# Squared key norms from the diagonal of k kᵀ on VectorE instead of TensorE transposes and ScalarE squares

## The chip, the cores and the metric

The kernel runs on one core of one Trainium2 chip. A core has five engines that work side by side and wait for one another through semaphores: TensorE (PE in the profile; its weight loads are PEld), VectorE (DVE), ScalarE (ACT), GpSimd (POOL) and SyncE (SP, which here issues DMAs). The metric is device time in microseconds (us), lower is better. TensorE writes its products to PSUM, eight banks of 512 fp32 values per partition; VectorE and ScalarE read them from there.

## The reference

The reference is one transformer block over 8 sequences of 256 tokens and 256 channels, all in fp32: a layer norm with a scale and shift from a conditioning vector, a gated delta-rule attention with 16 key heads and 32 value heads of width 128, then a second layer norm and a feed-forward part that keeps two of every four hidden values. Cut to what matters here:

```
qkv = x @ W_qkv.T ; z = x @ W_z.T ; beta = sigmoid(x @ W_b.T) ; decay = exp(-softplus(..) * exp(A_log))
q, k, v = causal convolution of qkv over 4 tokens, per channel
q, k = q / |q|, k / |k|                       # per token and key head
S = S * decay + k (beta * (v - k S))          # per token, two value heads to a key head
out = q S ; out = rmsnorm(out) * norm_w * silu(z) ; y = out @ W_out.T
```

The norm |k| that is to be computed is one number per token and key head: the root of the sum of 128 squares.

## The kernel before

The scan over tokens is done in chunks of 128 tokens. For each key head, two sequences and two chunks (so four 128x128 blocks), the kernel builds a triangular matrix from k kᵀ, the decays and beta / |k|², inverts it, and gets the outputs by matmuls. The heads go in groups of four, and the sequences in pairs: 4 pairs x 4 groups = 16 groups, 64 key heads in all.

The names that matter:

- `stage_a` (L479) makes one key head: `projected` (L429) multiplies the weights with the tokens into the PSUM tile `ps_k`; `convolved` (L417) makes `k_t` of it, one ScalarE and three VectorE instructions. `k_t` has channels on partitions and tokens along the free axis, so a sum over channels is a sum over partitions.
- `norms2` (L441) gives the squared norms. It transposes the four blocks on TensorE into a bank (`ps_n2k`), so that tokens are on partitions, and squares each on ScalarE with an accumulated sum (`junk`, L451). It serves the queries too (`n2q`).
- From the squared norms `n2` come a clamp (L500), a reciprocal (L505), `bk` = beta / |k|² (L507), and on GpSimd `diag` (L516), which puts `bk` on the diagonals of eight blocks, and `nk`, the norm (L523).
- Then k kᵀ, the tile `ps_kk` (L534), a scan over `dbc` (the decays, loaded by DMA) and `diag` into `e` (L553), and the product `a_t` = k kᵀ times `e` (L565). Four DMAs write the diagonal blocks of `a_t` to `scr` in DRAM (L574).
- `stage_b` (L582) loads the blocks of a whole group back (`blk`), and solves 32x32 blocks in 30 steps on VectorE (L599, L605). `levels` (L669) joins them to whole inverses on TensorE (`ps_w`, `ps_t`, `ps_w2`, `ps_t2`), `attend` (L759) computes the outputs, `prepare` (L614) queries, values and gates, `shares` (L894) the output projection, `feed_forward` (L160) the last part (`ps_ff`, `ps_out`).

The parts are Python generators. Each `yield` hands over to the next, and `along` (L1084) advances the next group's `stage_a` and `stage_b` while the present group attends. That gives a first order. From it a scheduler makes the final order on each engine when the program is built: earlier text has precedence, and an instruction that is not ready in its model lets later ones pass. So an edit in one place can shift the order elsewhere. [...]

PSUM is split in three pools: `ps_in` with three banks (`ps_k`, `ps_qv`, `ps_z`, `ps_y`, and the transposes of `norms2`), `ps_inv` with two (`ps_kk`, the four tiles of `levels`, `ps_ff`, `ps_out`), `ps_mix` with three for `attend`. A tile holds its bank from its first write until its last reader is done. `diag` has one buffer (pool `single`).

In the first group (`first`) nothing runs beside `stage_a`; there `e` is made in another way (L536 to L551).

## Time and profile before

| | |
|---|---|
| median of 3 runs | 2170.34 us (2168.94 to 2173.52) |
| profiled execution | 2170.51 us, span of the instructions 2168.7 us |
| mean granted TensorE clock | 0.991 of full speed |
| TensorE busy | 2068.7 us, 95% of the span |
| VectorE busy | 1669.4 us, 77% |
| ScalarE busy | 1379.5 us, 64% |
| GpSimd busy | 370.3 us, 17% |

The page lists busy time by engine, the chain of work that ended last, and groups of instructions by line, with the shape, the count, the busy time in us, the mean duration of one in ns, and the idle time of the engine just before them with what ended it. The durations of matmuls overlap, since they are pipelined. An ordinary fp32 matmul of this kernel stands in the trace as two records and a transpose as one: the 256 products of k kᵀ are 512 records, the 256 transposes of keys 256. The line numbers in the profile before are those of the code above.

### The profile page before, as it was taken

What the parts mean: (1) busy time and instruction counts of PE and PEld (TensorE: products, weight loads), DVE (VectorE), ACT (ScalarE), POOL (GpSimd) and SP (SyncE); (2) the same over time, 40 slices, a digit from 0 to 9 for tenths busy, and PEclk for the clock granted to TensorE, in tenths of its full rate; (3) what the DMA queues carried; (4) which work ended last, traced back from release to release, by engine and by line L of the source; (5) the groups of instructions that cost most, each with busy time, mean ns of one, the idle gap of its engine ahead of it and who ended that gap; (6) DMA issues with size and microseconds to landing.
All of it is one profiled execution on the core that took longest, in us unless ns stands there. A gap on an engine that the chain in (4) does not pass through costs nothing.

```text
span 2168.7 us, 46393 instructions
## 1 busy us (share of the span) xinstructions
PE 2068.7 (95%) x16684; PEld 1633.8 (75%) x16684; DVE 1669.4 (77%) x4039; ACT 1379.5 (64%) x4552; POOL 370.3 (17%) x375
## 2 busy tenths in 40 slices
PE   8889999899999999999999999999999999999998
PEld 5567777777777787777777787777778777777887
DVE  6678786787869587797877868787887868878457
ACT  3577677766656566665666656667666666666652
POOL 3120212112120211212121121211212021120010
PEclk9999999999999999999999999999999999999999
DMA  4242424223242443434334343433434244343226
GB/s 142 86 112 64 106 70 111 76 82 111 80 113 71 114 129 91 130 92 105 119 87 112 106 124 97 118 113 89 125 92 116 83 119 128 94 112 91 72 90 212
DMA packets 324517, 226.85 MB, mean 105 GB/s; under 512 B 254520, under 2 KB 266168, under 8 KB 324288
## 3 DMA queue, kind: packets, MB, share of 16 engines
q1 hardware_dynamic: 304416, 163.34, 28.0%
q10 hardware_dynamic: 19872, 60.54, 8.7%
q8 instruction: 133, 2.18, 0.4%
q14 instruction: 96, 0.79, 0.1%
HBM read 186.28 MB, written 29.12 MB: 99 GB/s over the span
## 4 chain that ended last, share of the span: by engine, by line
PE 50%; DVE 12%; DMA 7%; ACT 7%; issue 3%; POOL 1%; SPq 1%; DVEq 0%; ACTq 0%; POOLq 0%
PE ps_z L641 7%; PE ps_y L902 7%; PE ps_qv L432 6%; PE ps_ks L813 4%; PE ps_ff L190 3%; DVE cv L420 3%; DMA blk<-scr 2%; PE ps_o L832 2%; PE ps_out L244 2%; PE ps_k L432 2%; PE ps_u L848 2%; DMA scr<-a_t 2%; PE ps_u L805 1%; PE ps_o L854 1%; PE ps_gt L888 1%
## 5 line engine op out<-in xcount | busy, mean ns | idle before, releaser
L420 DVE SCALAR_TENSOR_TENSOR cv<-ps_qv,conv_sb,cv 128x510 f32<-128x510 f32 (+2 forms) x564 | 408.2, 735 | 29.8 <-ACT cv L418 28.2
L432 PE MATMUL ps_qv<-h_bp,wh 128*128 128x512 f32 x768 | 369.0, 605 | 20.5 <-DVE cv L420 8.0
L105 POOL TENSOR_TENSOR rs<-ss,minus_halves 128x4 f32<-128x4 f32 x128 | 134.3, 1055 | 1104.2 <-DVE ss L859 1096.9
L641 PE MATMUL ps_z<-wh,h_bp 128*128 128x256 f32 x1024 | 247.4, 386 | 10.6 <-ACT junk L451 7.4
L902 PE MATMUL ps_y<-wo,og_p 128*128 128x256 f32 x1024 | 236.1, 380 | 0.0
L432 PEld LDWEIGHTS ps_qv<-h_bp,wh 128*128 128x128 f32 x768 | 132.9, 191 | 125.3 <-issue 97.0
L641 PEld LDWEIGHTS ps_z<-wh,h_bp 128*128 128x128 f32 x1024 | 187.9, 192 | 38.5 <-ACT junk L451 9.6
L902 PEld LDWEIGHTS ps_y<-wo,og_p 128*128 128x128 f32 x1024 | 187.9, 190 | 22.3
L599 DVE TENSOR_TENSOR tmp<-blk,xb 128x30 f32<-128x30 f32 (+14 forms) x480 | 157.3, 328 | 51.2 <-ACT xb L593 41.7
L839 ACT ACTIVATE junk<-o 128x128 f32<-128x128 f32 x512 | 154.2, 306 | 54.8 <-DVE o L855 44.3
L516 POOL TENSOR_TENSOR diag<-consts,bk 128x1032 f32<-128x1032 f32 x64 | 122.8, 1918 | 364.1 <-DVE bk L507 364.1
L418 ACT ACTIVATE cv<-ps_qv,conv_sb 128x512 f32<-128x512 f32 x188 | 129.7, 690 | 82.8 <-PE ps_qv L432 81.4
L553 DVE TENSOR_TENSOR_SCAN e<-dbc,diag 128x1032 f32<-128x1032 f32 x60 | 138.0, 2300 | 37.1 <-POOL diag L516 35.5
L605 DVE TENSOR_TENSOR xb<-xb,tmp 128x30 f32<-128x30 f32 (+14 forms) x480 | 157.6, 328 | 9.5
L872 DVE SCALAR_TENSOR_TENSOR og<-o,rs,gz 128x128 f32<-128x128 f32 x512 | 146.2, 349 | 14.5 <-POOL rs L105 13.9
L420 DVE SCALAR_TENSOR_TENSOR k_t<-ps_k,conv_sb,k_t 128x510 f32<-128x510 f32 (+1 forms) x189 | 139.4, 739 | 20.6 <-ACT k_t L418 18.8
L813 PE MATMUL ps_ks<-u,cross 128*128 128x128 f32 x1024 | 141.3, 282 | 0.9 <-ACT u L807 0.9
L813 PEld LDWEIGHTS ps_ks<-u,cross 128*128 128x128 f32 x1024 | 132.1, 196 | 11.1 <-issue 4.8
L190 PE MATMUL ps_ff<-h,w_ff 128*128 128x128 f32 x1024 | 131.9, 278 | 3.3 <-ACT h L149 2.4
L779 ACT ACTIVATE vn<-ps_v,nk 128x256 f32<-128x256 f32 x256 | 104.0, 483 | 44.6 <-PE ps_v L774 44.1
L190 PEld LDWEIGHTS ps_ff<-h,w_ff 128*128 128x128 f32 x1024 | 123.1, 192 | 7.6 <-ACT h L149 3.3
L432 PE MATMUL ps_k<-h_bp,wk 128*128 128x512 f32 x256 | 122.3, 602 | 1.2 <-ACT junk L451 1.2
(177 smaller groups left out, 4280.1 us busy)
## 6 DMA issues: line engine op xcount, KB each, us to landing
wh<-in_w_heads ACTq DMA_DIRECT2D x64, 640.0 KB, 4.0
w_ff<-in_w_ff SPq DMA_DIRECT2D x128, 256.0 KB, 3.1
dbc<-d_dram SPq DMA_DIRECT2D x60, 516.0 KB, 4.6
wo<-in_w_heads ACTq DMA_DIRECT2D x32, 512.0 KB, 3.7
w_dn<-in_w_down SPq DMA_DIRECT2D x64, 256.0 KB, 3.3
wk<-in_w_keys SPq DMA_DIRECT2D x16, 512.0 KB, 4.9
scr<-a_t SPq DMA_DIRECT2D x256, 32.0 KB, 2.5
blk<-scr SPq DMA_DIRECT2D x16, 512.0 KB, 3.6
```

The source lines that it names most:

```text
L105: nc.gpsimd.tensor_tensor(out=out, in0=in_, in1=minus_halves[:, :n], op=ALU.pow)
L190: nc.tensor.matmul(ps[:, a, l, :], lhsT=w[:, k, l, :], rhs=h2[:, k, :], start=(k == 0), stop=(k == CC - 1),)
L420: nc.vector.scalar_tensor_tensor(out=dst[:, :, d:], in0=ps[:, :, : T - d], scalar=taps[:, KC - 1 - d : KC - d], in1=dst[:, :, d:], op0=ALU ...
L432: nc.tensor.matmul(ps.rearrange("p b t -> p (b t)"), lhsT=w[k], rhs=h_bp[:, k, :], start=(k == 0), stop=(k == CC - 1),)
L553: nc.vector.tensor_tensor_scan(e.rearrange("p i s t -> p (i s t)"), dbc.rearrange("p i f -> p (i f)"), diag.rearrange("p s t -> p (s t)"), ...
L599: nc.vector.tensor_tensor(out=tmp, in0=blk[:, j, j + 1 :, None].to_broadcast([P, m, j]), in1=xb[:, j, None, 0:j].to_broadcast([P, m, j]), ...
L605: solved = nc.vector.tensor_tensor(out=xb[:, j + 1 :, 0:j], in0=xb[:, j + 1 :, 0:j], in1=tmp, op=ALU.subtract)
L641: nc.tensor.matmul(ps[:, n, :], lhsT=h_bp[:, k, i * T + n * P : i * T + (n + 1) * P], rhs=wh[:, k * 640 + 384 : (k + 1) * 640], start=(k = ...
L813: nc.tensor.matmul(ps_ks[:, ct, h, :], lhsT=cross[:, h, ct, :], rhs=u0[:, h, :], start=True, stop=True)
L839: nc.scalar.activation(junk, o[:, n, h, :], AF.Square, accum_out=ss[:, n, h : h + 1])
L872: nc.vector.scalar_tensor_tensor(out=og[:, n, h, :], in0=o[:, n, h, :], scalar=rs[:, 2 * n + h : 2 * n + h + 1], in1=gz[:, i, n, h, :], op ...
L902: nc.tensor.matmul(ps_y[:, n, :], lhsT=og_p[:, j // 2, i, n, j % 2, :], rhs=wo[:, j // 2, j % 2, :], start=(j == 0), stop=(j == 3),)
```

## The change

k kᵀ of a head is computed ahead of its norm, for all heads. For the heads after the first group (60 of 64) the squared norms are read from its diagonal: VectorE multiplies the four blocks with the identity into the first part of `diag`'s buffer (`own`), and sums each row. The clamp, the reciprocal and all that follows are as they were, and GpSimd then overwrites the same buffer with the `diag` proper. The four heads of the first group keep `norms2`, and so do the queries. The tile `diag` is asked for earlier; its size and its one buffer are the same. `a_t` reads the same PSUM tile as before (`kk` is `ps_kk`).

```diff
             yield rec
-            n2 = norms2(k_t, "n2k")
+            ps_kk = bank(ps_inv, [P, 2 * NCH, P], "ps_kk")
+            for i in range(2):
+                for n in range(NCH):
+                    kc = k_t[:, i, n * P : (n + 1) * P]
+                    nc.tensor.matmul(ps_kk[:, i * NCH + n, :], lhsT=kc, rhs=kc, start=True, stop=True)
+            kk = ps_kk
+            diag = single.tile(
+                [P, 2 * NS, PE1], F32, tag="dbc" if first and kh % 2 else "diag", name="diag"
+            )
+            if first:
+                n2 = norms2(k_t, "n2k")
+            else:
+
+                n2 = small.tile([P, 2, NCH], F32, tag="n2k", name="n2k")
+                own = diag[:, : 2 * NCH, :P]
+                nc.vector.tensor_tensor(
+                    out=own, in0=kk, in1=ident[:, None, :].to_broadcast([P, 2 * NCH, P]), op=ALU.mult
+                )
+                nc.vector.tensor_reduce(
+                    out=n2.rearrange("p i n -> p (i n)"), in_=own, axis=AX.X, op=ALU.add
+                )
             nc.vector.tensor_scalar_max(n2, n2, L2_EPS2)
...
-            diag = single.tile(
-                [P, 2 * NS, PE1], F32, tag="dbc" if first and kh % 2 else "diag", name="diag"
-            )
             done = nc.gpsimd.tensor_tensor(
...
             rec["e"] = e
-            ps_kk = bank(ps_inv, [P, 2 * NCH, P], "ps_kk")
-            for i in range(2):
-                for n in range(NCH):
-                    kc = k_t[:, i, n * P : (n + 1) * P]
-                    nc.tensor.matmul(ps_kk[:, i * NCH + n, :], lhsT=kc, rhs=kc, start=True, stop=True)
...
-                    in0=ps_kk[:, i * NCH : (i + 1) * NCH, None, :].to_broadcast([P, NCH, 2, P]),
+                    in0=kk[:, i * NCH : (i + 1) * NCH, None, :].to_broadcast([P, NCH, 2, P]),
```

## The prediction

> **What bounds the kernel now.** I read the profile in this order: the engines' shares, the TensorE rows at close range, what TensorE waits for, the rows of the touched instructions, and the windows of one group of heads.

> ```profile
> PE 2068.7 (95%) x16684; PEld 1633.8 (75%) x16684; DVE 1669.4 (77%) x4039; ACT 1379.5 (64%) x4552; POOL 370.3 (17%) x375
> ```

> TensorE is the fullest, but its durations overlap, so 95% is not its real load. Start-to-start times tell that. In the timeline (start us, us, engine, line):

> ```profile
> 1000.86 0.29 ACT L451 ACTIVATE junk<-ps_n2k 128x128 f32<-128x128 f32 x1
> ...
> 1001.11 0.29 ACT L451 ACTIVATE junk<-ps_n2k 128x128 f32<-128x128 f32 x1
> ...
> 1008.54 0.60 PE L447 MATMUL ps_n2k<-consts,k_t 128*128 128x128 f32 x4
> ...
> 1008.98 1.04 PE L774 MATMUL ps_v<-consts,cv 128*128 128x128 f32 x8
> ```

> Four transposes start at 1008.54 and the next work at 1008.98: 0.11 us each, where the row says 0.277. One square with its accumulator read takes 0.25 us of ScalarE (1001.11 - 1000.86). In the same way 256 columns take 0.216 and 512 take 0.43. By records: 1,024 of 512 columns are 440 us, 2,560 of 256 are 553, some 6,650 of 128 are 739, the 32- and 64-wide ones about 140 in bursts, the rest 50: 1,923 us, 89% of 2168.7. So 11%, some 245 us, is not issue: about 1,000 steps of 0.1 us at semaphores, and named waits. The waits of TensorE (us, times, longest):

> ```profile
> PE ps_qv L432 <- DVE cv L420: 8.0, 7, 1.6
> PE ps_z L641 <- ACT junk L451: 7.4, 5, 3.6
> ...
> PE ps_qv L432 <- DVE k_t L420: 5.1, 6, 1.3
> ...
> PE ps_qv L432 <- DVE y L913: 4.2, 5, 1.1
> ...
> PE ps_qv L432 <- ACT junk L451: 3.0, 4, 0.9
> ```

> Summed over that whole view, TensorE waits some 36 us for VectorE, 47 for ScalarE and 10 for DMA. None is for a_t (L565), so today nobody on TensorE waits for the bank that k k^T sits in. The chain that ended last says the same:

> ```profile
> PE 50%; DVE 12%; DMA 7%; ACT 7%; issue 3%; POOL 1%; SPq 1%; DVEq 0%; ACTq 0%; POOLq 0%
> ```

> The kernel is bound by TensorE's issue, with VectorE second.

> [...]

> **The change, part by part.** These are the touched rows (busy us, mean ns, then idle before):

> ```profile
> L553 DVE TENSOR_TENSOR_SCAN e<-dbc,diag 128x1032 f32<-128x1032 f32 x60 | 138.0, 2300 | 37.1 <-POOL diag L516 35.5 <-POOL nk L523 0.9 <-DMA dbc<-d_dram 0.7
> ...
> L565 DVE TENSOR_TENSOR a_t<-ps_kk,e 128x512 f32<-128x512 f32 x128 | 81.9, 680 | 13.9 <-PE ps_kk L534 12.6 <-DMA t_inv<-scr_y 0.4
> ...
> L451 ACT ACTIVATE junk<-ps_n2k 128x128 f32<-128x128 f32 x256 | 68.9, 287 | 75.3 <-PE ps_n2k L447 74.8
> ...
> L447 PE MATMUL ps_n2k<-consts,k_t 128*128 128x128 f32 x256 | 39.7, 277 | 2.4 <-DVE k_t L420 2.4
> ```

> *Removed from TensorE.* 60 of the 64 key heads lose four transposes: 240 x 0.109 us (0.44 / 4) = 26.2 us, on the engine that sets the end: **-26**. The k k^T matmuls stay; they only move ahead.

> *Removed from ScalarE.* 240 squares with their reads, 240 x 0.25 = 60 us. ScalarE is at 64%, so most of it was hidden behind TensorE. What shows is TensorE waiting for a bank of ps_in that the squares still read: 7.4 + 3.0 + 1.2 = 11.6 us (L641, and L432 twice); the squares of keys and of queries share that line with 256 each, so half: **-6** (bounds 0 and -12). If ScalarE's relief shortens its other waits in proportion to its load (60 of 1,380), that is 2 more, left in the range.

> *Added to VectorE.* A product of 128x512 from PSUM and a sum of 128x512 from SBUF for each of 60 heads. The product is a_t's row, 680 ns; two of these run in 1.27 us at 1011.29, so the second starts 0.6 after the first. No sum over the free axis with this form stands in the trace. [...] What hides it is VectorE's idle time, 499 us before, 427 after. TensorE's 36 us of waits for VectorE, scaled with 499 / 427, grow by 6; with the two dependent steps of each pair **+7** (0 if it all falls in idle time; 72 if the cover is gone). Late next would be the convolutions (cv, k_t at L420), aq and rr, which are queued behind on VectorE and for which TensorE waits.

> *The chain of a head.* Before: transposes, squares, clamp, reciprocal, bk, GpSimd's diag (1.92 us), scan, a_t. In one head the transposes began at 513.03 and the squares were over at 516.49, 3.5 us. Now: k k^T 1.06 us, product and sum 1.4, about 2.5. The four writes to scr on SP's queue, the gather to blk and the solve follow a_t; no DMA is issued elsewhere in the queue by the edit. I count this as nothing: VectorE's queue ahead of the product replaces ScalarE's ahead of the squares.

> *A wait moved.* diag is one buffer, and it now holds the product too: the product of the next head cannot pass the previous head's scan. Both are on VectorE; queued behind it are those same convolutions. In the changed order the product often stands right behind the previous a_t, so its data is long there. Nothing counted.

> *The bank.* ps_kk now is held from ahead of the norm up to a_t. Pairing the instructions of the 60 heads in order of time, k k^T to the end of a_t takes 7.5 us on average, first transpose to the end of a_t 18.6. ps_inv has two banks, which levels and ps_ff share. In the changed program's order on TensorE, 13.9 us of issue on average (before: 9.2) stand between a head's k k^T and the next write to its bank; stretched by 2168.7 / 1928 this is 15.6 us of room. The chain needs about 1.0 + 1.4 + 9.1 (median from the clamp to the end of a_t, now) = 11.5, and in the slowest tenth some 19. It fits for most heads; six stalls of 0.5 us: **+3** (bounds 0 and 60 x 3.0, the gap between 18.6 and 15.6, = 180, if the long waits of today stayed, which mostly were waits for ScalarE).

> *The first four heads* keep the old norm, but eight k k^T records now run ahead of their transposes: 8 x 0.11 = 0.9 us each, in the start where TensorE waits: **+1.5** (0 to 3.6).

> Sum: -26.2 - 6 + 7 + 3 + 1.5 = -20.7. The profiled execution took 2170.51 us (span 2168.7, 1.8 outside it), the median of the runs is 2170.34, so both serve alike: 2170.5 - 20.7 = **2150 us**.

> **The rivals.** *VectorE becomes the bound (slower).* The windows of a group (length, then busy us of PE, PEld, DVE, ACT, POOL):

> ```profile
> 960.00:975.00 15.00, 14.23 (x101) 9.56 (x101) 12.82 (x35) 13.08 (x41) 2.25 (x3) 1.00 0.46 137
> 975.00:990.00 15.00, 15.00 (x189) 11.37 (x188) 10.84 (x19) 10.60 (x34) 2.90 (x2) 1.00 0.43 109
> 990.00:1005.00 15.00, 15.00 (x136) 14.13 (x135) 7.38 (x23) 10.21 (x47) 2.92 (x4) 1.00 0.42 99
> 1005.00:1020.00 15.00, 13.83 (x126) 9.88 (x124) 13.58 (x23) 7.34 (x22) 5.40 (x4) 1.00 0.47 138
> ```

> Key heads are made in these. In two of four VectorE has 1.4 to 2.2 us left of 15, and exactly there TensorE isn't full. If the new pair lands in front of a convolution there, its 1.2 us reach TensorE whole. It decides from the point where more than 32 of the 72 us (45%) do so; with 70%, 50 us: 2170.5 - 32 + 50 = **2188**. Against it: the windows between have 4 to 7 us free, and VectorE's 12% of the chain is small beside TensorE's 50%.

> *TensorE's gain is not on the path.* The chain of waits runs through a_t, scr, blk and the solve in each group; if that sets a group's length, 26 us turn into waiting, and the moved waits cost a few: **2168**. Against it: in the solve TensorE hardly waits at all.

> *ScalarE's relief is worth more.* All 11.6 us of waits for L451 and 4 more go, VectorE hides everything: 2170.5 - 26 - 12 - 4 = **2129**.

> **How the numbers follow.** Likeliest 50% (its own range 2138 to 2162), VectorE 28%, not on the path 14%, more relief 8%. A measurement of this kernel can tell about 0.2% (4.3 us). Faster: 50 + 8 + 2 of the 14 = 60%; same: 10 of the 14; slower: 28 + 2. The range leaves out the lower half of the best case and the upper part of the worst: 2130 to 2196.

> **What would show it.** Right: ps_n2k at 16 records, TensorE's busy share some 2% of the span lower or the span shorter with the share kept; product and sum at about 680 ns each; L451's waits on TensorE halved; no TensorE wait for a_t. Wrong: TensorE's waits for VectorE (cv, k_t, aq) well above 36 us, waits of ps_w, ps_t or ps_ff for a_t, or a sum of over 1 us.

## The result, and the profile after

The changed kernel takes **2199.88 us** (median of 5 runs, 2194.66 to 2204.37); the kernel before, in runs beside it, 2170.34 us (2168.94 to 2174.33). The ratio is **1.0127**, 95% interval 1.0105 to 1.0149: some 28 us slower, where 2150 (range 2130 to 2196) and a gain were forecast. The profiled execution of the changed kernel took 2204.37 us (span 2202.6), at a mean granted TensorE clock of 0.971 against 0.991 before.

The engines of the changed kernel (busy us, share of the span, instructions):

```profile
PE 2067.1 (94%) x16444; PEld 1628.8 (74%) x16444; DVE 1754.0 (80%) x4159; ACT 1312.4 (60%) x4070; POOL 382.1 (17%) x375
```

240 TensorE records fewer, 120 VectorE instructions more, ScalarE relieved by 67 us, VectorE with 85 us more where 72 were forecast: each engine's work moved much as forecast. The touched groups (busy us, mean ns of one, idle before it):

```profile
L565 DVE TENSOR_TENSOR_SCAN e<-dbc,diag 128x1032 f32<-128x1032 f32 x60 | 137.9, 2298 | 33.8 <-POOL diag L533 33.6
...
L577 DVE TENSOR_TENSOR a_t<-ps_kk,e 128x512 f32<-128x512 f32 x128 | 81.9, 678 | 0.7
...
L514 DVE TENSOR_TENSOR diag<-ps_kk,consts 128x512 f32<-128x512 f32 x60 | 41.1, 685 | 26.5 <-PE ps_kk L503 26.5
L517 DVE TENSOR_REDUCE n2k<-diag 128x4 f32<-128x512 f32 x60 | 41.0, 683 | 1.1
...
L447 PE MATMUL ps_n2k<-consts,k_t 128*128 128x128 f32 x16 | 2.5, 280 | 0.0
```

One product and one sum cost what the prediction said. The loss is not in the length of the instructions, so I looked at the waits. Those of TensorE (us, times, longest):

```profile
PE ps_u L817 <- DVE aq L807: 21.1, 19, 2.2
...
PE ps_w L710 <- DMA x_even<-scr_x: 7.3, 4, 3.9
PE ps_t L764 <- DMA low_up<-t_inv: 7.0, 11, 1.7
...
PE ps_qv L432 <- DVE cv L420: 4.9, 3, 2.6
...
PE ps_qv L432 <- ACT junk L451: 2.4, 3, 0.8
```

L451's waits shrank as forecast (over all its lines from 11.6 us to 4.1), and those for the convolutions too. New is the first row: `attend` waits 19 times for `aq`, 21.1 us where it was 2.7, and the joins of the inverses wait for their DMAs. By my start-to-start sum over the trace, an estimate, TensorE's issue at full clock fell by 26 us (1,928 to 1,902), so the removed work did go. Its waits, summed over this whole view, rose from 95 us (99 times) to 129 (133 times): those for VectorE from 36 to 51, those for DMAs from 10 to 30, while those for ScalarE stayed at 47 and 46. No row of it is a wait for the bank of k kᵀ: TensorE's order is fixed when the program is built, and k kᵀ simply stands later in it. The chain that ended last has shifted from TensorE towards VectorE and DMA:

```profile
PE 41%; DVE 31%; DMA 10%; ACT 8%; issue 6%; POOL 2%; SPq 1%; ACTq 0%; DVEq 0%; POOLq 0%
```

**One head before and after.** The timelines show why (start us, us, engine, line). This is the first head of the ninth group in the kernel before; its `k_t` is finished by the first row:

```profile
969.22 0.74 DVE L420 SCALAR_TENSOR_TENSOR k_t<-ps_k,conv_sb,k_t 128x506 f32<-128x506 f32 x1
...
974.41 0.60 PE L447 MATMUL ps_n2k<-consts,k_t 128*128 128x128 f32 x4
...
979.38 0.16 DVE L507 TENSOR_TENSOR bk<-beta,rk 128x8 f32<-128x8 f32 x1
...
991.40 1.16 PE L534 MATMUL ps_kk<-k_t 128*128 128x128 f32 x8
992.60 1.29 DVE L565 TENSOR_TENSOR a_t<-ps_kk,e 128x512 f32<-128x512 f32 x2 [1.09 <-PE ps_kk L534]
```

The same head in the changed kernel:

```profile
988.62 0.74 DVE L420 SCALAR_TENSOR_TENSOR k_t<-ps_k,conv_sb,k_t 128x506 f32<-128x506 f32 x1
...
1009.25 0.69 PE L724 MATMUL ps_t<-t_inv,w 32*32 32x32 f32 x32
...
1009.87 1.16 PE L503 MATMUL ps_kk<-k_t 128*128 128x128 f32 x8
1011.07 0.69 DVE L514 TENSOR_TENSOR diag<-ps_kk,consts 128x512 f32<-128x512 f32 x1 [0.64 <-PE ps_kk L503]
1011.79 0.69 DVE L517 TENSOR_REDUCE n2k<-diag 128x4 f32<-128x512 f32 x1
...
1013.83 0.16 DVE L527 TENSOR_TENSOR bk<-beta,rk 128x8 f32<-128x8 f32 x1
...
1018.36 1.29 DVE L577 TENSOR_TENSOR a_t<-ps_kk,e 128x512 f32<-128x512 f32 x2
```

In both kernels k kᵀ starts some 20 us after `k_t`, behind the joins of the group before (`ps_t` at 1009.25), which use the same two banks of `ps_inv`. Before, the norm did not care: its transposes had a bank of `ps_in` 4.5 us after `k_t`, and `bk`, `diag` and the scan were long done when k kᵀ came, so `a_t` followed at once and ended 23.9 us behind `k_t`. Now the norm begins only there, and the whole chain hangs behind k kᵀ: `a_t` ends 30.3 us behind `k_t`. The means over the 15 later groups, from the end of `k_t` to the end of `bk`, in us (first to fourth head of a group): 10.0, 31.6, 28.0, 8.7 before; 25.6, 32.6, 34.7, 8.2 after. From the first `ps_k` of a group to its last `a_t`: 73.3 before, 79.7 after. That is the theory tested below, called R: **the norm is late because it has been tied to a bank of `ps_inv`.** Its rivals carry these letters in the expectations:

- V: the added VectorE work is too much for VectorE.
- B: k kᵀ holds its bank for longer, or the shifted order costs.
- P: TensorE's removed work was never on the path. A: ScalarE without the squares runs ahead and crowds VectorE.
- Q: the pair (product and sum) stands in front of `aq` in VectorE's queue. O: any shift of the scheduler's order gives another time, without a sign.
- D: the shared buffer `diag` makes the product wait. L: a norm that goes through VectorE's queue is late, wherever its data is.

### The profile page after: what moved, and what is told of

It reads as the page before. It is cut to its first block, busy times and chain, and to the rows that moved or that the text cites. A ratio compares the mean times of both kernels' runs of the same rounds, so it can differ in the third digit from the quotient of the medians.

```text
span 2202.6 us, 45564 instructions
## 1 busy us (share of the span) xinstructions
PE 2067.1 (94%) x16444; PEld 1628.8 (74%) x16444; DVE 1754.0 (80%) x4159; ACT 1312.4 (60%) x4070; POOL 382.1 (17%) x375
## 4 chain that ended last, share of the span: by engine, by line
PE 41%; DVE 31%; DMA 10%; ACT 8%; issue 6%; POOL 2%; SPq 1%; ACTq 0%; DVEq 0%; POOLq 0%
DVE cv L420 7%; PE ps_z L653 6%; PE ps_qv L432 5%; PE ps_y L914 4%; PE ps_ks L825 3%; DVE a_t L577 3%; DMA blk<-scr 3%; PE ps_ff L190 2%; DVE e L565 2%; PE ps_out L244 2%; DVE og L884 2%; DMA scr<-a_t 2%; DMA low_up<-t_inv 2%; DVE xb L617 2%; DVE tmp L611 2%
## 5 line engine op out<-in xcount | busy, mean ns | idle before, releaser
L420 DVE SCALAR_TENSOR_TENSOR cv<-ps_qv,conv_sb,cv 128x510 f32<-128x510 f32 (+1 forms) x564 | 408.1, 737 | 19.5 <-ACT cv L418 17.8
L432 PE MATMUL ps_qv<-h_bp,wh 128*128 128x512 f32 x768 | 381.4, 621 | 7.8 <-DVE cv L420 4.9
L105 POOL TENSOR_TENSOR rs<-ss,minus_halves 128x4 f32<-128x4 f32 x128 | 148.5, 1168 | 810.2 <-DVE ss L871 785.8
L914 PE MATMUL ps_y<-wo,og_p 128*128 128x256 f32 x1024 | 240.9, 384 | 5.9 <-ACT gz L660 4.0
L432 PEld LDWEIGHTS ps_qv<-h_bp,wh 128*128 128x128 f32 x768 | 136.1, 197 | 109.0 <-issue 95.9
L653 PEld LDWEIGHTS ps_z<-wh,h_bp 128*128 128x128 f32 x1024 | 185.4, 191 | 39.7 <-issue 6.3
L420 DVE SCALAR_TENSOR_TENSOR k_t<-ps_k,conv_sb,k_t 128x510 f32<-128x510 f32 (+2 forms) x189 | 139.2, 739 | 36.4 <-ACT k_t L418 34.4
L565 DVE TENSOR_TENSOR_SCAN e<-dbc,diag 128x1032 f32<-128x1032 f32 x60 | 137.9, 2298 | 33.8 <-POOL diag L533 33.6
L884 DVE SCALAR_TENSOR_TENSOR og<-o,rs,gz 128x128 f32<-128x128 f32 x512 | 155.2, 365 | 10.9 <-POOL rs L105 10.2
L825 PE MATMUL ps_ks<-u,cross 128*128 128x128 f32 x1024 | 146.5, 288 | 4.0 <-ACT u L819 2.1
L432 PE MATMUL ps_k<-h_bp,wk 128*128 128x512 f32 x256 | 121.8, 601 | 1.2 <-ACT junk L451 1.2
```

Of the source, the lines that this page charges most:

```text
L105: nc.gpsimd.tensor_tensor(out=out, in0=in_, in1=minus_halves[:, :n], op=ALU.pow)
L420: nc.vector.scalar_tensor_tensor(out=dst[:, :, d:], in0=ps[:, :, : T - d], scalar=taps[:, KC - 1 - d : KC - d], in1=dst[:, :, d:], op0=ALU ...
L432: nc.tensor.matmul(ps.rearrange("p b t -> p (b t)"), lhsT=w[k], rhs=h_bp[:, k, :], start=(k == 0), stop=(k == CC - 1),)
L565: nc.vector.tensor_tensor_scan(e.rearrange("p i s t -> p (i s t)"), dbc.rearrange("p i f -> p (i f)"), diag.rearrange("p s t -> p (s t)"), ...
L653: nc.tensor.matmul(ps[:, n, :], lhsT=h_bp[:, k, i * T + n * P : i * T + (n + 1) * P], rhs=wh[:, k * 640 + 384 : (k + 1) * 640], start=(k = ...
L825: nc.tensor.matmul(ps_ks[:, ct, h, :], lhsT=cross[:, h, ct, :], rhs=u0[:, h, :], start=True, stop=True)
```

## The experiments

Ratios are to the kernel before, run beside each kernel on the same chip, with 95% intervals. "`bk` of the first head" is the mean time from the end of `k_t` to the end of `bk` in the first heads of the 15 later groups. In e2, g2 and h1 the true norms are left out, as said there; all other kernels compute the whole reference.

### Parts of the change alone

**e1_kk_first**: the kernel before with k kᵀ and `diag` moved ahead of the norm, as in the change, and the old norm kept.

```diff
+            ps_kk = bank(ps_inv, ...)   # and its four matmuls, and diag
             n2 = norms2(k_t, "n2k")
...
-            ps_kk = bank(ps_inv, ...)   # and its four matmuls
```

> Only the move: k k^T ahead of the norm for all heads, with the old transposes and squares kept for all 64. Theory V (VectorE: the added pair makes TensorE wait in the stretches where key heads are made, and the granted clock falls behind those waits) expects no loss, 2165 to 2180 us and a granted clock near 0.99, since VectorE's work is unchanged. Theory B (bank and order: holding ps_inv longer, or the shifted order, costs) expects most of the loss here already, 2190 to 2205 us, with TensorE waiting for a_t ahead of ps_w, ps_t or ps_ff.

Measured 2172.55 us, 0.9993 (0.998 to 1.0006). Moving k kᵀ in the text costs nothing: with the norm in `ps_in`, `bk` of the first head still ends 10.5 us after `k_t`. Although its text now stands first, k kᵀ still starts only 19.2 us after `k_t` (21.7 before). It holds its bank for 11.7 us on average, from its start to the end of `a_t`, where before it was 7.5; that costs nothing either, so B falls.

**e2_no_norm**: the changed kernel without product and sum; the clamp reads a column of k kᵀ in their place, so the norms are left out, but they still depend on k kᵀ.

```diff
-                nc.vector.tensor_tensor(out=own, in0=kk, ...)
-                nc.vector.tensor_reduce(...)
-            nc.vector.tensor_scalar_max(n2, n2, L2_EPS2)
+                nc.vector.tensor_scalar_max(n2.rearrange("p i n -> p (i n)"), kk[:, :, 0], 1.0)
```

> The changed kernel without the product and the sum: for the 60 heads behind the first group the clamp reads one column of k k^T, so their norms are left out. It keeps the early k k^T and the removed transposes and squares. V expects the removal's gain in full, 26 us of TensorE issue and some waits: 2130 to 2150 us. B expects no gain, 2165 to 2195. A theory P (TensorE's removed work was never on the path) expects 2160 to 2172.

Measured 2167.93 us, 0.997 (0.9956 to 0.9984). So the pair is worth 0.0157 x 2170 = 34 us, give or take 6, where it stands in the change. But V expected 2130 to 2150 here. And with TensorE's 26 us gone, ScalarE relieved and VectorE spared, the gain is still only 6.5 us: something else eats 20. `bk` is late here too (21.8 us for the first head).

**e3_both**: e1, with product and sum added beside the old norm, their result unused.

```diff
             n2 = norms2(k_t, "n2k")
+            if not first:
+                nc.vector.tensor_tensor(out=own, in0=kk, ...)
+                nc.vector.tensor_reduce(out=n2x..., in_=own, ...)
```

> The changed kernel with the old transposes and squares put back for all heads, the product and the sum executed beside them with their result unused: VectorE's added work without what the change removes. V expects more than the changed kernel, 2205 to 2245 us (2170 plus 30 to 72), and VectorE waits on TensorE well above those of before. B expects what the move alone gives (within 5 us of that run). P expects 2200, the same as the changed kernel.

Measured 2171.09 us, 0.9983 (0.9972 to 0.9993). The same 120 instructions on VectorE, 82 us by their rows, cost nothing against e1 when no norm waits for them. This speaks against V as plain load. And k kᵀ holds its bank for 13.8 us on average here, 13.4 in the changed kernel, so the long hold isn't the cause of the loss.

**e4_transposes** and **f1_squares**: the changed kernel with the removed work put back, unused: 240 transposes of `k_t` on TensorE, or 240 squares of `k_t` on ScalarE.

```diff
+                ps_tr = bank(ps_in, [P, 2, NCH, P], "ps_tr")
+                for i in range(2):
+                    for n in range(NCH):
+                        nc.tensor.transpose(ps_tr[:, i, n, :], k_t[:, i, n * P : (n + 1) * P], ident)
```

> The changed kernel with the 240 transposes put back on TensorE, read by nobody (no squares). If TensorE's issue still sets the time, the 26 us come back in full: 2220 to 2230. V, with TensorE waiting for VectorE in just these stretches, expects part of them to fill those waits: 2200 to 2215, and a higher granted clock than 0.971, since TensorE has more to do in the thin windows. P expects 2200.

> The changed kernel with 240 squares put back on ScalarE for pacing alone (of k_t itself, result unused), and no transposes. The product and sum on VectorE still make the norm. Theory A (without the squares ScalarE runs ahead, its first convolution steps hand work to VectorE earlier, and this stands in front of aq, for which TensorE waits) expects 2165 to 2180 us, with more work than the changed kernel has. Theory O (the loss belongs to the order that the scheduler came to, and any shift of it gives another time between some 2150 and 2215) expects some other value, without a sign. Theory V in its first form (the pair's own time) expects 2200 or more, since nothing is taken from VectorE.

e4: 2212.06 us, 1.0181 (1.0166 to 1.0196); f1: 2204.07 us, 1.0172 (1.0141 to 1.0203). Against the changed kernel's 1.0127 that is some 12 us, give or take 6, for 26 us of TensorE issue, and some 10 us, give or take 8, for 60 us of ScalarE. So TensorE's relief is a gain even here, and P falls; A, which expected f1 to be faster, falls too. That ScalarE's relief is a gain is likely, not shown: g1 below lies 7 us above the changed kernel with no added work.

### Where the pair runs, and when

**f2_later**: product and sum one step later in the text. **f3_act_sum**: the sum on ScalarE, four accumulations, in place of VectorE's. **f4_pool_diag**: k kᵀ copied to SBUF by ScalarE, which frees its bank, then the product and two halvings on GpSimd, and a small sum on VectorE.

```diff
-                nc.vector.tensor_reduce(...)                                  # f3
+                for c in range(2 * NCH):
+                    nc.scalar.activation(junk, own[:, c, :], AF.Copy, accum_out=...)
...
+                nc.scalar.copy(kk_sb, ps_kk)                                  # f4
+                nc.gpsimd.tensor_tensor(out=own, in0=kk_sb, in1=ident..., op=ALU.mult)
+                for w in (P // 2, P // 4):
+                    nc.gpsimd.tensor_tensor(out=own[:, :, :w], in0=own[:, :, :w], in1=own[:, :, w : 2 * w], op=ALU.add)
```

> The changed kernel with the product and everything behind it handed over one step later in the text (the extra yield, which stood behind diag, now stands between k k^T and the product); the same instructions, none more or less. The product now comes behind the next round of attention, aq among it, in precedence. A theory Q (the pair stands in front of aq in VectorE's queue, and each such wait also costs a stretch at half clock) expects TensorE's waits for aq to go from 21 us to under 8 and the time to 2165 to 2185. O expects a shift of 10 us or more without a sign. V expects 2195 to 2205.

> The changed kernel with the sum moved to ScalarE (four accumulating copies of the product, 128 columns each, from SBUF): VectorE has 0.6 us a head less, ScalarE as much as before the change. V expects half of the loss: 2180 to 2190. A expects 2160 to 2175, since ScalarE is paced as before. Q expects 2180 to 2195 (the product still stands ahead of aq, half as long). O has no sign.

> k k^T copied to SBUF by ScalarE (one copy of 128x512 a head), the product and two halvings on GpSimd, only a sum of 128x128 on VectorE (about 0.3 us); a_t reads the copy, so the bank of ps_inv is free early. The 240 transposes stay away. V and Q expect the gain of TensorE's 26 us to show: 2145 to 2165. A expects 2160 to 2185 (ScalarE has half of its former pacing). If GpSimd's chain of three more instructions (some 3 us a head) is what sets the key heads' end, 2200 or more.

f2: 2197.13 us, 1.0142 (1.0114 to 1.0171), no change; nor did TensorE's waits for `aq` (20.3 us), so it doesn't test Q. f3 does: there these waits fall to 8.4 us, and it is slower all the same. f3: 2243.71 us, 1.0353 (1.0327 to 1.0378). f4: 2284.03 us, 1.0529 (1.0502 to 1.0557). Taking work *off* VectorE makes the kernel slower still, which V cannot explain. In these kernels the time rises with the length of a group's chain, from the first `ps_k` to the last `a_t`: 73.5 us in e2, 79.7 in the changed kernel, 86.1 in f3, 89.1 in f4, for 0.997, 1.0127, 1.0353 and 1.0529. f3 and f4 load other engines too, so their sizes prove less than their order, and the length is no measure for all runs: it is 76.8 us in e3 at 0.9983 and 75.3 in i1 at 1.0088. `bk` of the first head sorts them better: 10.0 to 12.4 us in the kernel before, e1, e3 and h1, which lose nothing, 24.1 to 33.2 in the changed kernel, e4, f1 to f4, g1 and i1, which all lose.

**g1_own_buffer**: the product in a buffer of its own, not in `diag`'s. **g2_no_norm_diag**: e2 with the clamp written through `diag`'s buffer, so that the shared buffer is waited for and the pair is not executed (norms left out).

```diff
-                own = diag[:, : 2 * NCH, :P]
+                own = single.tile([P, 2 * NCH, P], F32, tag="own", name="own")   # g1
...
+                four = diag[:, 0, : 2 * NCH]                                     # g2
+                nc.vector.tensor_scalar_max(four, kk[:, :, 0], 1.0)
```

> The changed kernel with one edit: the product goes to a buffer of its own (512 values a partition), no longer into diag's. Theory D (the product has to wait for the previous head's scan, the last reader of the one diag buffer, so product, sum, clamp, reciprocal and bk of the heads of a group stand in one chain with scan and a_t, where before only GpSimd's diag did) expects the loss to go: 2150 to 2178 us, with less time between a head's k k^T and its product for the third head (5.9 us on average in the changed kernel). Theory L (each hop through VectorE's queue delays the head, whatever the buffer) and V expect 2192 to 2205.

> The run without the norm (2168 us: one clamp reads a column of k k^T, product and sum left out), with that clamp written through the first four values of diag's buffer and a second one of four values to n2: 0.17 us more VectorE a head, and the wait for the previous scan. D expects a good part of the loss without any product or sum: 2180 to 2195. L and V expect no more than 2165 to 2173.

g1: 2205.18 us, 1.0159 (1.014 to 1.0179); g2: 2161.36 us, 0.9952 (0.9935 to 0.997). A buffer of its own doesn't help and the shared one doesn't hurt: D falls. O finds no support: the shifts of order in e1, e3 and h1 leave the time of the kernel before within 0.2%, and those in f2 and g1 that of the changed kernel within 0.4%.

### The bank

**h1_dve_norm**: the kernel before, with its transposes in `ps_in`, its late k kᵀ, and VectorE's product and sum (of the transposes) in place of ScalarE's squares; the values of the norms are left out. **h2_kk_in_ps_in**: the changed kernel, with k kᵀ of the 60 heads in a bank of `ps_in`.

```diff
+                ps_tr = bank(ps_in, [P, 2 * NCH, P], "ps_tr")        # h1
+                ... nc.tensor.transpose(ps_tr[:, i * NCH + n, :], ...)
+                nc.vector.tensor_tensor(out=own, in0=ps_tr, ...)
+                nc.vector.tensor_reduce(...)
...
-            ps_kk = bank(ps_inv, [P, 2 * NCH, P], "ps_kk")            # h2
+            ps_kk = bank(ps_inv if first else ps_in, [P, 2 * NCH, P], "ps_kk")
```

> The kernel before with one swap, at the old place: the transposes of the keys stay in their bank of ps_in, but VectorE's product and sum stand for ScalarE's squares (the product is with the identity, so the norm is not that of the reference; the instructions and shapes are the changed kernel's), k k^T stays late. Theory R (in the changed kernel the norm must wait until k k^T gets a bank of ps_inv, which the levels and the feed-forward hold; before, it went through ps_in early, 10 us behind the first head's keys in place of 26) expects no loss: 2160 to 2180 us, although VectorE has 72 us more and ScalarE 60 less. Theory L (a norm that goes through VectorE's queue is late, wherever its data is) and V expect 2192 to 2210.

> The changed kernel with one edit: k k^T of the 60 heads takes a bank of ps_in (three banks, from which the key transposes are gone) in place of ps_inv. R expects the norm of a group's first head back at 10 to 14 us behind its keys, and 2150 to 2180 us, unless the long hold of k k^T (13 us on average) starves the projections, which share ps_in: then TensorE's waits at ps_qv, ps_z and ps_y grow and the time stays above 2190. L and V expect 2192 to 2205.

h1: 2172.59 us, 0.9992 (0.9977 to 1.0006). h2: 2178.86 us, 1.003 (1.0013 to 1.0047). The engines of h1:

```profile
PE 2078.1 (96%) x16684; PEld 1639.0 (76%) x16684; DVE 1728.2 (80%) x4159; ACT 1317.0 (61%) x4071; POOL 363.8 (17%) x375
```

h1 has every VectorE instruction of the change, at the same 80%, and TensorE's full old work, and loses nothing: VectorE is no bound while the norm is early (`bk` of the first head 12.4 us after `k_t`), and a norm through VectorE's queue is not late by that: L falls. (ScalarE's squares are gone here; what that gives may hide a part of the pair's cost, but not in e3, which keeps them.) h2 differs from the changed kernel in the bank alone: k kᵀ now starts 4.4 us after `k_t` (21.3 in the changed kernel), `bk` ends at 12.0, and 21 of the 28 us are gone. The same head in h2:

```profile
982.98 0.74 DVE L420 SCALAR_TENSOR_TENSOR k_t<-ps_k,conv_sb,k_t 128x506 f32<-128x506 f32 x1
...
988.17 1.06 PE L503 MATMUL ps_kk<-k_t 128*128 128x128 f32 x8
```

**i1_norm_in_inv**: the kernel before, with nothing changed but the pool of the keys' transposes.

```diff
-            ps = bank(ps_in if name == "n2k" else ps_in, [P, 2, NCH, P], f"ps_{name}")
+            ps = bank(ps_inv if name == "n2k" and paced else ps_in, [P, 2, NCH, P], f"ps_{name}")
```

> The kernel before with one change: for the 60 heads after the first group the transposes of the keys take their bank from ps_inv in place of ps_in. TensorE's and ScalarE's work and VectorE's stay as before; nothing is added to VectorE. If the lateness of the norm at a bank of ps_inv is by itself enough for the loss (R), the norm now waits for levels and feed-forward again, and the time is 2190 to 2205, with bk of the first head of a group some 10 us later after k_t than in the kernel before. If the loss needs VectorE's added pair (V) or the longer hold of the bank of k k^T, it is 2168 to 2176. The transposes hold a bank of ps_inv only until the squares are done, some 2 to 4 us, so a part of the loss (2178 to 2190) would say that lateness and the long hold share it.

Measured 2191.76 us, 1.0088 (1.0055 to 1.0122). The same head in this kernel; its `k_t` ends at 972.17:

```profile
992.55 0.66 PE L447 MATMUL ps_n2k<-consts,k_t 128*128 128x128 f32 x4
...
996.51 0.17 DVE L507 TENSOR_TENSOR bk<-beta,rk 128x8 f32<-128x8 f32 x1
996.53 1.06 PE L534 MATMUL ps_kk<-k_t 128*128 128x128 f32 x8
...
1001.13 1.29 DVE L565 TENSOR_TENSOR a_t<-ps_kk,e 128x512 f32<-128x512 f32 x2
```

The transposes come 20 us after `k_t` where they came after 4.5, `bk` of the first head ends at 24.1 us on average, and 0.88% of 2172, **19 us**, are lost with the same instructions on every engine. This is R without the pair. The transposes are one tile more in `ps_inv`, but with 3.5 us of hold on average, and k kᵀ with 6.1, a head holds its banks for less than in e3, which lost nothing; that the extra turn itself costs something is not excluded. It fits e2 as well: -26 + 19 = -7, and e2 measured -6.5.

### More banks for `ps_inv`

**i2_three_inv** gives the changed kernel a third bank of `ps_inv` from `ps_in` (2, 3, 3 for `ps_in`, `ps_inv`, `ps_mix`), **j1_inv3_mix2** from `ps_mix` (3, 3, 2); **j2_before_inv3_mix2** is the kernel before in the split of j1.

```diff
-    ps_inv = ctx.enter_context(tc.tile_pool(name="ps_inv", bufs=2, space=PSUM))
+    ps_inv = ctx.enter_context(tc.tile_pool(name="ps_inv", bufs=3, space=PSUM))
```

> The changed kernel with one bank of PSUM moved from ps_in to ps_inv (two and three instead of three and two). If the wait of k k^T for a bank of ps_inv is the cause (R), the norm is early again and the time falls to 2150 to 2185, unless projections, which now have two banks, starve: then bk is early (the first head of a group within 15 us of k_t) and the waits of TensorE for the convolutions grow by tens of us. If the bank is not the cause, bk of the first head stays at some 25 us after k_t and the time at 2195 or above.

> The changed kernel with one bank moved from ps_mix (attend) to ps_inv: three banks for ps_in as before, three for ps_inv, two for ps_mix. If the bank of ps_inv is the cause (R), bk of the first head comes some 10 us earlier than in the changed kernel and, if attend lives with two banks, the time falls below before: 2140 to 2170. If attend starves, the time rises above 2200 with TensorE's waits at ps_u, ps_o, ps_ks; the companion run of the kernel before in the same split tells what the split itself costs.

> The kernel before with the same split of banks (3, 3, 2). It is the price of the split by itself: 2165 to 2180 if attend lives with two banks, above 2200 if it starves. Under R the loss of the change in this split (j1 against j2) is smaller than its 1.3% in the split of the program, or a gain; if the bank is not the cause, it stays at 1 to 1.5%.

i2: 2273.01 us, 1.0465 (1.0431 to 1.0498). j1: 2291.49 us, 1.0535 (1.0503 to 1.0568). j2: 2345.3 us, 1.0792 (1.0757 to 1.0827). In i2 the norm does come earlier (`bk` of the first head at 16.6 us, of the third at 20.0 where it was 34.7), but the other pools cannot spare a bank: TensorE's waits before projections are 45 us where the changed kernel has 20, and in j1 those in `attend` 80 where it has 48. The hope of a version faster than both fell. With three banks in `ps_inv` the change itself gains, 54 us from j2 to j1, as R expected, but not by an early norm: `bk` of the first head ends at 22.0 us in j1, not 10 us earlier than 25.6 as expected, and at 17.9 in j2. So this pair is no evidence for R.

**j3_own_kk**: the kernel before, with the norms from a k kᵀ of their own in `ps_in`, product and sum on VectorE, and a second, late k kᵀ in `ps_inv` for `a_t`.

```diff
+                ps_nn = bank(ps_in, [P, 2 * NCH, P], "ps_nn")
+                ... nc.tensor.matmul(ps_nn[:, i * NCH + n, :], lhsT=kc, rhs=kc, start=True, stop=True)
+                nc.vector.tensor_tensor(out=own, in0=ps_nn, ...)
+                nc.vector.tensor_reduce(...)
```

> The kernel before with its key norms from a k k^T of their own in a bank of ps_in (product and sum on VectorE in a buffer of their own, no transposes, no squares of keys), and the k k^T for a_t late in ps_inv as before. The norms are early and the pair on VectorE is paid; TensorE pays 240 products of about 0.22 us in place of 240 transposes of 0.11, 26 us more than before. If TensorE's issue sets the end as the prediction has it, 2190 to 2202; if issue is half hidden, as the put-back transposes suggest, 2175 to 2190. Under V (VectorE's pair) it would be higher than 2200.

Measured 2193.38 us, 1.009 (1.0064 to 1.0117), with `bk` of the first head at 12.2 us. Against the kernel before, 26 us of TensorE issue more cost 19.5 us, with ScalarE's relief and the pair in that. h1 is the closer comparison, since it differs in the products alone: 1.009 - 0.9992, some 21 us. When the norm is early, TensorE's issue comes through for the most part.

## Why the prediction was wrong, step by step

**The steps that failed are "The chain of a head" and "The bank".** The first counted the move of the norm behind k kᵀ as nothing, because "VectorE's queue ahead of the product replaces ScalarE's ahead of the squares". It compared lengths of work, 2.5 us against 3.5, and not the starts: k kᵀ stood 21.7 us behind `k_t` in the trace before, the transposes 4.5 in the head shown. The second looked at who waits for the bank that k kᵀ *holds*, and there it was about right: the hold is 13.4 us on average after, in a room of 15.6, and TensorE waits 0.3 us for `a_t`. It never asked what k kᵀ waits for to *get* the bank, since nothing hung on that before but `a_t`. Lateness costs 19 us without the pair (i1), where both steps together had +3.

**VectorE's pair, +7**, had its durations right (685 and 683 ns forecast as 680) and its place wrong. No run shows the 1.2 us a head, 72 us in all, that stand behind the +7 and the rival's 2188: they were my estimate, which put the product's 0.60 us on the sum too; the runs showed 41.1 us for 60 products and 41.0 for 60 sums, and VectorE 85 us busier. Off the chain (e3) or early in it (h1) it costs nothing. In a chain that has become late it costs 34 us (e2 against the change). The sum is -26 + 19 + 34 = +27 us, and 0.0127 x 2170 = 28 were measured. This is a weak check: the 34 is itself the changed kernel less e2 and contains whatever goes with the pair, the interval of the 19 reaches from 12 to 26, and -26 for TensorE without ScalarE closes no better than the -12 and -10 of e4 and f1.

**TensorE, -26**, was right in size: 1,928 to 1,902 us of issue; put back in the late chain, 12 us of it show (e4), and in an early one 21 us of a like amount (j3 against h1). **ScalarE, -6**, was right within f1's reach (10, give or take 8). **The moved wait for `diag`, nothing**, was right (g1, g2). **The first four heads, +1.5**: `k_t` of the next group's first head ends 1.0 us later (95.41 against 94.39).

**Of the rivals**, VectorE as the bound gave 2188, and the prediction had named `aq` among what would be late next, which is what TensorE waits for. One of two windows in the late stretch shows VectorE almost full (length, then busy us of PE, PEld, DVE, ACT, POOL, then the clock):

```profile
1010.00:1025.00 15.00, 15.00 (x140) 14.27 (x141) 11.02 (x28) 9.99 (x43) 5.12 (x5) 1.00 0.45 103
1025.00:1040.00 15.00, 13.24 (x95) 9.47 (x93) 14.69 (x28) 7.20 (x16) 3.21 (x2) 1.00 0.53 155
```

But h1 carries the same pair for nothing, so its mechanism fell: VectorE seems short of time only where late heads crowd. The gain that is not on the path (2168) and more relief (2129) are far off.

**Left open.** h2 has the early norm, the pair and 26 us less on TensorE, and yet is 6.5 us slower than before; by the terms above it should gain. Its k kᵀ holds a bank of `ps_in` for some 12 us (988.17 to 1000.88 in this head) where the transposes held one for 2.3 (974.41 to 976.73); on average it is 12.4 against 7.2. i2 shows that banks of `ps_in` are dear. But the projections, which would starve, show no such waits: TensorE's waits before them are 24 us in h2 and 32 before. Those at the joins of the inverses grew, from 10 to 40 us, most of all for `x_even` by DMA (13.1 us). Why is open. Also, TensorE's waits land on other lines in i1 (`ps_u` for `vn`, 13.7 us) than in the change (`aq`): which wait a late head turns into is decided by the order that the scheduler makes, and was not traced further.

## What to carry to other kernels

When a result is to be read from something that already exists, look up when that thing comes to exist, not only what reading it costs: the start in the trace before, of the new source against the old one (here 21.7 us behind `k_t` on average against 4.5 in the head shown), for the slowest heads of a group. In this kernel the PSUM pool is part of a value's dependencies: in i1 the transposes of that head, with their bank from `ps_inv`, started 20 us behind `k_t` in place of 4.5, and 19 us were lost with the same instructions on every engine. The pair, 82 us by its rows, was free off the chain (e3) and in an early chain (h1), and cost 34 us in the late chain of the change, some two fifths.

## What the runs showed of the hardware

In the changed kernel a stall of TensorE was followed by a stretch at a granted clock of 0.50. `aq` is late behind the product, two convolutions and the sum on VectorE, and `ps_u` waits 1.76 us for it:

```profile
1036.10 0.68 DVE L514 TENSOR_TENSOR diag<-ps_kk,consts 128x512 f32<-128x512 f32 x1
...
1036.70 0.73 DVE L420 SCALAR_TENSOR_TENSOR cv<-ps_qv,conv_sb,cv 128x510 f32<-128x510 f32 x1
...
1037.35 0.67 DVE L517 TENSOR_REDUCE n2k<-diag 128x4 f32<-128x512 f32 x1
...
1037.95 0.73 DVE L420 SCALAR_TENSOR_TENSOR cv<-ps_qv,conv_sb,cv 128x508 f32<-128x508 f32 x1
...
1038.60 0.68 DVE L807 TENSOR_TENSOR aq<-ps_kq,e 128x512 f32<-128x512 f32 x1
...
1039.33 0.71 PE L817 MATMUL ps_u<-vn,t_inv 128*128 128x128 f32 x4 [1.76 <-DVE aq L807]
...
1040.06 3.64 PE L432 MATMUL ps_qv<-h_bp,wh 128*128 128x512 f32 x4
```

The windows around it, cut at the clock's changes at 1040.00 and 1043.41 and, ahead of them, in steps of the same 3.41 us (columns as above; the clock stands behind POOL):

```profile
1033.17:1036.59 3.42, 3.42 (x25) 2.29 (x25) 3.42 (x8) 2.33 (x6) 0.00 (x0) 1.00 0.51 157
1036.59:1040.00 3.41, 1.65 (x38) 1.27 (x36) 3.41 (x8) 1.99 (x5) 0.00 (x0) 1.00 0.37 62
1040.00:1043.41 3.41, 3.40 (x5) 1.18 (x4) 3.41 (x8) 0.37 (x1) 0.56 (x1) 0.50 0.00 0
```
